# Two buffers for a turned tile, longer landing times in the plan, and a new order, in a kernel of four graph layers

## The chip, the cores and the metric

The kernel runs on one core of a Trainium2 chip. The metric is the device time of one execution in microseconds, the median of several runs. An execution that the hardware profiler recorded gives the profile; its own time is stated beside it.

## The reference

64 graphs of 256 nodes, each with 256 features in f32 and an integer adjacency matrix of 256 x 256. Four layers follow each other, and each ends in a residual sum and a layer norm. Cut to what is computed:

```python
# layer 0: attention with 8 heads over edges in either direction, then a feed-forward of width 1024
allowed = (adj > 0) | (adj.T > 0) | eye
q, k, v = split(x @ Wqkv.T + bqkv)
ctx = softmax(where(allowed, (q * scale) @ k.T, -inf)) @ v          # per head
x1 = layernorm(x + ctx @ Wo.T + bo)
y = layernorm(x1 + relu(x1 @ W1.T + b1) @ W2.T + b2)
x = layernorm(x + y)
# layers 1 and 2: graph attention, masked by adj (elu behind the second)
h = x @ W
e = leaky_relu(f[:, None] + g[None, :])                             # f = h @ a1, g = h @ a2
x = layernorm(x + softmax(where(adj > 0, e, -big)) @ h)
# layer 3: two graph convolutions over the edges of type 1, elu behind each
h = elu(x @ w_root + b + (adj == 1).T @ x / deg @ w_rel)            # twice
x = layernorm(x + h)
```

## The kernel before, in words

One graph is one unit of work: two tiles of 128 nodes. TensorE does the products, ScalarE exponentials and many evacuations of PSUM, VectorE masks, sums and statistics, POOL (GpSimd) a small root for each layer norm and DMAs that add, and SP (SyncE) issues the other DMAs.

**A plan sets the order of everything.** `main_path` doesn't issue instructions. It records operations in a `Plan`: setup as graph 0's first part, then `graph(g)` for each of the 64 graphs. Each operation has an engine, a cost in us, the tiles that it reads and writes and, on TensorE, a mode ("full", "row" for the 32-row score products, "col" for the values, "one" for gathering, "turn"). `Plan.schedule` then plays the operations through against these costs and puts them in order. An operation that moves data has a size and a `lag`, the time to landing. What is played decides only the order of issue; on the chip semaphores decide when things run.

**What the plan goes by.** Each kind of operation has a due time in `DUE`, and each graph a shift in `LATER`, about 41.12 us from one graph to the next; the sum is the operation's key. An engine takes, among its operations that are ready, the one with the smallest key. `WORTH` says how much the key is changed where a change of mode on TensorE would be saved or paid, `HOLD` how long TensorE may wait for a better operation, `WINDOW` how far ahead of its queue's head an operation may be taken. A pair of score groups is tied in `attention`: behind the first TensorE may be held for the second, for a time that `LOCK` sets. `RINGS` says how many buffers each kind of tile has; when all are in use the operation has to wait, in the plan and on the chip.

**How a tile is turned.** TensorE needs the features on the partitions. Except for the last five graphs, `bounced` does this without TensorE: VectorE transposes blocks of 32 x 32 into the tile `turned` (L839), SP sends that to DRAM (`rows`, L842, 256 KB, landing time `SENT` in the plan), and SP fetches it back in another order into a tile `T` (L847, landing time `BACK`). There are five such round trips in each graph: ahead of the feed-forward, of each attention layer and of each convolution. `turned` is free again once the send has landed. In the last five graphs `turned` is instead the scratch of a ScalarE copy (L828) ahead of a transpose on TensorE; in the first two graphs it serves the input. A column of the attention layers, f, is spread over all partitions in a like manner by `f_on_all`: `row<-cols` (L1102, `SENT_ROW`), then `pf<-row` (L1104, `BACK_ROW`), and VectorE uses it at L1134. `bits_bounced` turns the adjacency bits with the same two constants as `bounced`.

**Places that the steps touch.** The function `product`, at L888, issues all "full" products; the tile names tell them apart: `w,hid` is the second feed-forward product, `T,w` the first, `wo,ctxT` the output product, `gw,T` and `h,e` the attention layers, `cw,T` the convolutions. Scores are L1006, values L1041 and L1046, gathering L1208. PSUM has eight banks, a ring named `bank`: each product takes one, a score group takes four, and VectorE or ScalarE frees it by evacuating, for instance at L1067 behind the output product and the second feed-forward product.

Of the kernel before, what the change touches and what calls it, by code (L numbers as in the profile page):

```python
# [29 lines left out]
SENT, BACK = 2.5, 3.0  # L30
SENT_ROW, BACK_ROW = 2.7, 3.7
# [3 lines left out]
         "xr": 1, "hid": 1, "h": 3, "e": 3, "n": 1, "rel": 3, "hi": 2, "lo": 2, "o": 4, "blocks": 1, "turned": 1, "xT": 2, "cols": 2, "pf": 2, "turned_b": 1, "pt": 1}  # L35
# [4 lines left out]
WORTH, HOLD, WAIT, LOCK = 19.5, 0.38, 1000000.0, -0.5  # L40
WINDOW, FIRST, TAIL = 4.08, 6, 58
LANES = 8
DUE = [
    -3.32, 1.66, -76.45, -66.99, 176.19, 125.8, -337.49, 51.11, -306.84, 1289.72, 1238.75, 106.05, 1052.79, 157.6, 406.79, 32.53, 320.05, 308.78, 168.26, 372.3,
    359.81, 399.94, 414.94, 175.34, -771.48, 577.65, -163.58, 38.1, 102.4, 97.86, 212.59, 174.98, 232.55, 216.55, 274.84, 330.62, 335.24, 134.38, 316.14, 312.12,
    -714.12, 335.95, 93.11, 1673.19, 1202.97, 341.42, -15.89, 342.83, 413.55, 332.78, 471.02, 386.89, 1310.89, 1011.01, 864.41, 1559.09, 1349.75, 1637.58, 532.45, 391.77,
    408.67, 281.04, 416.08, 267.08, 455.95, 205, 355.16, 826.3, 430.38, 916.11, 855.23, 1541.74, 1480.45, 874.17, 97.88, -356.53, -611.17, -654.7, -556.93, 187.88,
    -58.31, -599.7, -1620.93, -1008.29, -941.93, 172.6, -1279.24, -1141.77, -510.52, -858.89, -979.24, -122.59, -551.6, -53.94, 320.94, 661.97, 122.99, 710.02, 442.1, 806.71,
    803.71, 196.79, 28.84, -268.67, 974.73, 412.51, 222.77, -44.51, 850.39, 787.86, 941.67, 355.66, -240.36, 390.1, 131.66, 324.9, -400.33, -177.96, -449.86, 87.86,
    479.23, 133.36, -458.92, 481.3, 336.71, 363.47, 57.85, -169.97, 1025.83, -703.56, 453.78, 429.72, -683.8, 94.09, -397.82, -779.14, -1443.53, -1281.14, -485.56, -330.59,  # L50
    -509.36, -1319.48, -919.17, -897.92, -285.58, -961.77, 42.95, 1101.45, 539.68, 510.97, -335.37, -103.6, -174.06, -1101.15, -1331.4, -1100.65, -427.55, -1096.38, -584.1, -528.48,
    302.19, -1032.08, -330.62, 813.25, 398.18, 877.77, 398.14, 1710.52, 243.46, -201.85, -604.71, 278.16, -763.26, -1414.9, -851.67, -2262.54, -1880.07, -2413.17, -1323.08, -993.79,
    -1535.67, -693.92, -857.19, -1680.81, -1238.83, -1544.75, -1551.8, -934.32, -665.58, 92.11, 250.88, 278.27, 1064.42, 556.25, 1200.96, 835.73, -229.1, 11.51, -1287.5, -719.39,
    491.11, -340.67, 297.98, 1036.71, 331.46, 935.5, 1276.44, 543.66, 635.98, -233.76, -236.54, -143.35, -85.56, 690.47, -1128.24, -188.51, 229.9, -337.83, -470.47, 303.07,
    294.95, -1177.63, -332.74, 497.93, 141.48, -1379, -1116.01, -852.76, -415.54, -805.34, -233.53, -85.67, -596.8, 398.69, 696.99, 36.47, 229.51, 513.36, 314.46, -844.71,
    -684.07, -952.69, -715.38, -939.59, -374.49, -1092.97, -2.92, -325.51, 48.64, 255.67, -499.52, -317.02, 498.86, 236.78, -987.53, -782.88, -696.09, -1493.47, 626.47, -425.51,
    328.26, 844.48, 40.56, -366.7, -664.35, -542.74, -715.91, -174.14, -819.33, -520.44, -852.66, 44.87, 87.36, -682.13, -510.83, 668.23, 127.3, -187.38, -1280.09, -1206.13,
    -1236.51, -626.27, -1017.5, -1329.36, -1426.82, -1567.82, -1426.23, -1356.52, -2016, -2549.52, -1764.4, -2044.6, -2365.67, -2132.03, -2998.04, -2021.84, -2693.01, -1477.56, -1450.67, -437.11,
    -1066.87, -1380.6, -1185.68, -1912.99, -1175.82, -162.05, -1388.62, -687.93, -841.24, -198.9, -255.02, 93.71, -418.45, -510.09, -139.81, 47.47, 135.24, 486.36, 940.09, 106.41,
    6.92, -142.92, -12.02, -979.84, -87.84, -965.42, -1781.15, -2113.16, -1887.77, -1185.84, -637.88, -1423.79, -566.06, -662.98, -128.84, -369.82, -195.94, -48.52, -1090.36, -444.68,  # L60
    -388.84, -151.83, 145.45, 234.1, 760.1, 257.54, -733.81, -429.47, 364.12, 792.5, -314.71, 646.77, -164.87, 701.44, 928.18, -19.63, 1261.73, 319.26, 612.03, 411.07,
    135.41, 335.64, -108.85, -486.71, -806.72, -566.65, -449.1, 43.21, -260.78, -477.86, -196.66, -58.56, 623.95, 663.12, -261.97, 184.16, -238.39, -199.48, 99.86, -71.13,
    -605.68, -363.77, -860.86, -278.1, 48.25, -322.31, -227.04, 52.9, -93.63, 752.97, -375.97, 104.87, 638.78, -464.01, 152.82, -357.39, -133.36, -172.46, -693.73, -319.61,
    -1412.19, -571.28, 21.04, -355.31, -767.51, -91.62, 338.07, -307.97, 256.87, 424.85, 725.57, -10.94, 461.61, -537.13, 230.24, 44.85, 169.31, -632.54, -605.49, 344.21,
    52.37, 61.16, -784.38, -840.31, -1510.97, -1387.71, -326.58, 0.5, -2.81, -445.54, -785.65, 159.28, -390.96, -339.72, -869.93, -460.79, -402.39, -246.94, -415.89, 172.83,
    17.22, 692.89, 140.89, 573.8, 162.6, 1080.8, 453.49, -61.94, 656.12, 203.45, 326.3, 632.37, 318.61, 358.35, 726.28, -221.2, 1220.66, 405.08, 364.19, -345.95,
    -118.89, -92.68, 12.95, -117.23, -118.43, 150.37, -31.48, 210.98, 66.46, 139.57, 130.65, 250.91, 77.66, 45.65, -90.38, 146.96, 120.09, 223.68, 302.85, 191.15,
    38.27, 121.41, 77.94, 257.82, 100.58, 94.11, 43.37, 414.45, 47.32, 244.3, 134.83, -56.21, 3.74, 101.61, 88.73, 107.62, 44.63, 75.98, 208.29, 120.2,
    76.84, 38.88, 124.51, -51.9, 57.61, -15.19, 219.49, 37.59, 238.22, 38.45, 165.9, 71.58, 103.5, 92.26, 36.02, 89.94, 114.24, 161.76, 136.12, 155.43,
    144.91, 136.25, 123.82, 173.19, 37.23, 54.94, 104, 351.37, 393.87, 420.97, 398.66, 329.73, 309.87, 376.83, 322.26, 357.45, 228.89, 342.28, 396.51, 264.8,  # L70
    409.7, 283.52, 331.27, 163.63, 197.2, 321.78, 181.03, 106.22, 172.35, 191.86, 363.79, 199.39, 154.03, 196.39, 365.08, 208.79, 166.91, 204.19, 148.9, 150.92,
    244.16, 201.73, 216.8, 205.05, 129.18, 306.33, 270.33, 298.69, 352.43, 242.1, 109.35, 149.21, -104.34, -63.72, 176.35, 97.62, 67.93, 247.43, 42.64, 224.12,
    197.04, 150.42, 99.42, 237.34, 203.98, 307.4, 319.2, 195.63, 311.24, 340.21, 420.84, 405.34, 295.63, 432.84, 393.88, 333.09, 378.89, 470.14, 353.74, 66.9,
    326.36, 491.34, 433.25, 443.86, 355.61, 304.99, 415.15, 458.93, 251.59, 519.13, 458.87, 384.71, 402.37, 377.98, 354.25, 449.89, 251.68, 289.09, 424.6, 414.09,
    405.23, 416.12, 379.79, 392.18, 370.61, 497.61, 394.33, 438.45, 405.63, 365.46, 396.94, 387.75, 400.37, 298.4, 408.37, 356.47, 404.89, 394.43, 352, 379.31,
    394.41, 251.56, 336.68, 302.2, 284.86, 400.44, 341.02, 509.96, 449, 481.19, 495.26, 517.82, 671.2, 389.86, 450.74, 491.74, 629.85, 444.94, 844.35, 203.63,
    11.32, 5.91, 0.56, 6.63, 27.83, 5.07, 14.09, 14.62, 28.08, 28.56, 51.27, 77.51, 59.49, 92.29, 98.75, 143.06, 30.76, 31.95, 39.6, 40.28,
    92.74, 93.6, 94.67, 95.03, 73.53, 76.62, 100.59, 105.53, 113.1, 113.3, 106.82, 109.59, 106.36, 108.11, 110.88, 116.61, 106.61, 107.98, 114.11, 109.72,
    111.49, 108.56, 113.73, 103.81, 119.66, 124.56, 124.37, 122.99, 122.52, 126.54, 125.24, 131.28, 134.46, 141.05, 142.97, 145.22, 145.49, 142.26, 209.5, 149.61,
    150.68, 151.53, 151.6, 152.66, 154.61, 171.25, 185, 155.74, 156.35, 160.25, 172.83, 187.04, 165.58, 166.44, 167.51, 166.87, 169.97, 172.59, 174.9, 174.38,  # L80
    173.45, 174.79, 175.86, 176.22, 167.3, 168.52, 174.02, 174.74, 177.85, 183.58, 187.56, 190.38, 196.2, 189.39, 200.1, 201.11, 203.16, 203.82, 201.61, 211.08,
    212.34, 221.15, 234.26, 238.23, 237.07, 238.97, 252.57, 296.8, 239.41, 241.4, 243.2, 250.85, 249.69, 251.34, 247.91, 253.96, 258.76, 258.67, 253.08, 254.17,
# [1444 lines left out]
```

## Time and profile before

| what | value |
|---|---|
| runs | 2748.38, 2755.47, 2757.27 us; median 2755.47 |
| profiled execution | 2746.21 us, span 2744.4 us |
| granted TensorE clock, mean | 0.995 |
| TensorE busy | 2695.8 us (98%), 15152 matmul records |
| VectorE busy | 2360.0 us (86%) |
| ScalarE busy | 1529.7 us (56%) |
| POOL busy | 1181.0 us (43%) |
| rows<-turned and T<-rows | 295 DMAs of 256 KB each |
| moved by DMA | 425.35 MB, 155 GB/s in the mean |

A stretch of the profile gives, for each engine, its busy time and in brackets its number of instructions. A group of waits gives the engine and line that waited, what ended the wait, the us in total, the times and the longest. The chain is the work that ended last, followed back from the end; in order of time each piece has its start, its length and what it was. A name such as `DMA pf<-row` in it is the time from a DMA's issue to its landing. "PEld" are TensorE's weight loads. A matmul of f32 leaves two records in the trace, so a score group of eight matmuls shows as x16.

### The profile page before, as it was taken

To read this page: it belongs to the slowest core of one execution; us is meant where nothing else is said; L and a number is where in the kernel's file an instruction comes from. 1 tells how busy PE (TensorE), PEld (TensorE's weight loads), DVE (VectorE), ACT (ScalarE), POOL (GpSimd) and SP (SyncE) were. 2 spreads that over 40 slices of the span, in tenths; PEclk is the share of its full clock that TensorE was granted. 3 is DMA by queue.
4 is the path that set the end of the run, shared out by engine and by line. 5 is a ranking of instruction groups with operands and counts; after the bars stand their busy time and mean duration, and the time that the engine had idled before them with its cause. 6 is when DMAs were issued, how large, how long until landed. Compare 5 with 4: busy or idle time off the path is not lost.

```text
span 2744.4 us, 48371 instructions
## 1 busy us (share of the span) xinstructions
PE 2695.8 (98%) x15152; PEld 2092.1 (76%) x15152; DVE 2360.0 (86%) x6585; ACT 1529.7 (56%) x3830; POOL 1181.0 (43%) x2051
## 2 busy tenths in 40 slices
PE   7999999999999999999999999999999999999997
PEld 5887777777777777777877777877777777777774
DVE  5688989889889898889898898898898898988767
ACT  4445555555555555555555555555555655556667
POOL 2443344344444444444444454444444444434222
PEclk9999999999999999999999999999999999999999
DMA  7786777577786786786776777777777877786221
GB/s 189 151 166 140 163 164 168 126 155 159 166 175 155 166 175 154 167 174 154 172 173 152 168 169 163 168 165 163 171 160 159 174 155 168 159 198 142 63 50 40
DMA packets 801742, 425.35 MB, mean 155 GB/s; under 512 B 552078, under 2 KB 777384, under 8 KB 801480
## 3 DMA queue, kind: packets, MB, share of 16 engines
q1 hardware_dynamic: 720504, 291.46, 41.1%
q0 software_dynamic: 80976, 130.72, 29.8%
q8 instruction: 124, 2.03, 0.3%
q14 instruction: 138, 1.13, 0.1%
HBM read 190.46 MB, written 102.09 MB: 107 GB/s over the span
## 4 chain that ended last, share of the span: by engine, by line
PE 65%; DVE 17%; DMA 9%; issue 3%; ACT 3%; POOL 2%; SPq 1%; DVEq 0%; ACTq 0%; POOLq 0%
PE bank L888 54%; DMA rows<-turned 4%; PE bank L1006 4%; DMA pf<-row 3%; PE bank L1208 3%; PE bank L1046 3%; DVE fold L1023 2%; DVE p L1014 2%; DVE turned L839 2%; PE bank L1041 1%; DVE e L1134 1%; DVE st L897 1%; ACT X L909 1%; DVE lo L1196 1%; DVE mv L899 1%
## 5 line engine op out<-in xcount | busy, mean ns | idle before, releaser
L902 POOL TENSOR_SCALAR rstd<-mv 128x2 f32<-128x2 f32 x384 | 135.9, 354 | 1041.2 <-DVE mv L899 918.0
L888 PE MATMUL bank<-T,w 128*128 128x256 f32 x2048 | 479.9, 380 | 1.1 <-DVE rdeg L1214 0.6
L888 PE MATMUL bank<-w,hid 128*128 128x256 f32 x2048 | 466.1, 382 | 1.8 <-ACT hid L1084 1.8
L888 PE MATMUL bank<-cw,T 128*128 128x512 f32 x1024 | 463.7, 593 | 2.6 <-DMA cw<-in_w_root_dram 1.1
L909 ACT ACTIVATE X<-X,rstd 128x256 f32<-128x256 f32 x640 | 350.1, 599 | 204.2 <-POOL rstd L905 196.0
L1012 ACT ACTIVATE p<-bank 128x512 f32<-128x512 f32 x512 | 300.4, 605 | 264.6 <-PE bank L1006 264.3
L888 PEld LDWEIGHTS bank<-w,hid 128*128 128x128 f32 x2048 | 396.3, 196 | 63.5 <-issue 21.5
L888 PEld LDWEIGHTS bank<-T,w 128*128 128x128 f32 x2048 | 382.5, 190 | 71.1 <-issue 21.8
L1014 DVE TENSOR_TENSOR p<-p,am 128x512 f32<-128x512 f32 x512 | 336.0, 679 | 8.8 <-ACT p L1012 8.0
L1084 ACT ACTIVATE hid<-bank,col_b 128x256 f32<-128x256 f32 x512 | 215.3, 472 | 225.7 <-PE bank L888 225.5
L888 PEld LDWEIGHTS bank<-cw,T 128*128 128x128 f32 x1024 | 198.3, 195 | 183.3 <-issue 164.6
L903 POOL TENSOR_TENSOR rstd<-rstd,neghalf 128x2 f32<-128x2 f32 x384 | 316.1, 823 | 32.3
L1029 POOL DMA_DIRECT2D fold<-p x240 | 204.9, 870 | 156.0 <-DMA fold<-p 65.8
L888 PE MATMUL bank<-xT,wqkv 128*128 128x256 f32 x1024 | 260.4, 383 | 1.2 <-DVE xT L880 0.8
L888 PE MATMUL bank<-h,e 128*128 128x259 f32 x1024 | 254.9, 382 | 2.6 <-ACT e L1139 0.9
L888 PE MATMUL bank<-gw,T 128*128 128x258 f32 x1024 | 254.1, 380 | 0.3 <-DMA T<-rows 0.3
L839 DVE STREAM_TRANSPOSE turned<-X 128x512 f32<-128x512 f32 x236 | 166.8, 707 | 101.8 <-DMA rows<-turned 86.9
L888 PEld LDWEIGHTS bank<-gw,T 128*128 128x128 f32 x1024 | 199.4, 195 | 49.3 <-issue 17.1
L897 DVE BATCH_NORM_STATS2 st<-X 128x6 f32<-128x256 f32 x640 | 234.5, 407 | 0.8
L888 PEld LDWEIGHTS bank<-h,e 128*128 128x128 f32 x1024 | 192.1, 190 | 38.1 <-issue 2.8
L888 PEld LDWEIGHTS bank<-xT,wqkv 128*128 128x128 f32 x1024 | 190.9, 191 | 32.8 <-issue 5.9
L1195 ACT CAST hi<-bank 128x256 fp32r<-128x256 f32 x256 | 93.1, 364 | 220.0 <-PE bank L888 219.2
(159 smaller groups left out, 4774.4 us busy)
## 6 DMA issues: line engine op xcount, KB each, us to landing
rows<-turned SPq DMA_DIRECT2D x295, 256.0 KB
T<-rows SPq DMA_DIRECT2D x295, 256.0 KB
fold<-p POOLq DMA_DIRECT2D x240, 256.0 KB, 5.0
adj<-in_adj_dram SPq DMA_DIRECT2D x128, 256.0 KB
x<-in_x_dram SPq DMA_DIRECT2D x64, 256.0 KB
xr<-in_x_dram SPq DMA_DIRECT2D x64, 256.0 KB
x<-row_bo POOLq DMA_DIRECT2D x64, 256.0 KB, 7.7
X<-row_b POOLq DMA_DIRECT2D x64, 256.0 KB, 6.5
```

The lines of the kernel that those rows point to most:

```text
L839: dve(0.63, lambda: nc.vector.transpose(turned().rearrange("p k (b n i) -> p (k b) i n", b=4, i=NB), xt().rearrange("p i (j c) -> p j i c" ...
L888: nc.tensor.matmul(dst, lhsT=lhs(c), rhs=rhs(c), start=(c == 0), stop=(c == n - 1))
L897: nc.vector.bn_stats(stat()[:, i, :], y()[:, i, :])
L902: nc.gpsimd.tensor_scalar(rstd()[:, 0, :], mv()[:, :, 1], 1.0, EPS, op0=ALU.mult, op1=ALU.add)
L903: nc.gpsimd.tensor_tensor(rstd()[:, 0, :], rstd()[:, 0, :], neghalf[:, 0:NB], op=ALU.pow)
L909: nc.scalar.activation(y()[:, i, :], y()[:, i, :], AF.Identity, bias=rstd()[:, 1, i : i + 1], scale=rstd()[:, 0, i : i + 1])
L1006: nc.tensor.matmul(s[r]()[:, hg, :], lhsT=qk()[f, KB + hg, kt * P : (kt + 1) * P], rhs=qk()[f, hg, :], start=True, stop=True)
L1012: act(0.58, lambda pr=pr, k=k, sr=s[r]: nc.scalar.activation(pr(), sr(), AF.Exp, accum_out=seen_sum[:, k : k + 1]), [s[r]], [(p[kt], r)])
L1014: dve(0.60, lambda pr=pr, kt=kt: nc.vector.tensor_tensor(pr(), pr(), am()[:, kt, None, :].to_broadcast([P, KB, N]), op=ALU.mult), [(p[kt], ...
L1029: op("POOL", 1.3, lambda kt=kt, hg=hg, into=into, out_of=out_of: nc.gpsimd.dma_start(fold()[into], p[kt]()[out_of, hg], accum_op=ALU.add), ...
L1084: act(0.36, lambda f=f, k=k, ph=ph: nc.scalar.activation(hid()[:, f + k, :], ph()[:, k, :], AF.Relu, bias=b1[:, f + k : f + k + 1]), [ph, ...
L1195: act(0.27, lambda i=i, po=po: nc.scalar.copy(hi()[:, i, 0:D], po()[:, D:]), [po], [(hi, i)])
```

## The change

The ring of `turned` gets two buffers in place of one. The landing times that the plan uses grow: `SENT` from 2.5 to 3.5 us, `BACK` from 3.0 to 4.0, `SENT_ROW` from 2.7 to 3.0, `BACK_ROW` from 3.7 to 5.0. `WORTH`, `HOLD` and `WINDOW` get other values, and all of `DUE` (one number for each kind of operation) and `LATER` (one for each graph) are replaced. No function changes. The core of the diff:

```diff
-SENT, BACK = 2.5, 3.0
-SENT_ROW, BACK_ROW = 2.7, 3.7
+SENT, BACK = 3.5, 4.0
+SENT_ROW, BACK_ROW = 3.0, 5.0
...
-         "xr": 1, "hid": 1, "h": 3, "e": 3, "n": 1, "rel": 3, "hi": 2, "lo": 2, "o": 4, "blocks": 1, "turned": 1, "xT": 2, "cols": 2, "pf": 2, "turned_b": 1, "pt": 1}
+         "xr": 1, "hid": 1, "h": 3, "e": 3, "n": 1, "rel": 3, "hi": 2, "lo": 2, "o": 4, "blocks": 1, "turned": 2, "xT": 2, "cols": 2, "pf": 2, "turned_b": 1, "pt": 1}
...
-WORTH, HOLD, WAIT, LOCK = 19.5, 0.38, 1000000.0, -0.5
-WINDOW, FIRST, TAIL = 4.08, 6, 58
+WORTH, HOLD, WAIT, LOCK = 18.26, 0.66, 1000000.0, -0.5
+WINDOW, FIRST, TAIL = 3.87, 6, 58
...
 DUE = [
-    -3.32, 1.66, -76.45, -66.99, 176.19, 125.8, -337.49, 51.11, -306.84, 1289.72, 1238.75, 106.05, 1052.79, 157.6, 406.79, 32.53, 320.05, 308.78, 168.26, 372.3,
+    -5.24, 61.16, -55.48, -121.71, 131.27, 116.42, -360.14, -13.03, -412.23, 1303.25, 1202.5, 122.94, 1220.77, 264.52, 518.37, 26.62, 302.48, 323.95, 108.43, 382.73,
...
 LATER = [
-    -295.85, -398.08, 82.34, 186.95, 93, 148.02, 240.73, 287.76, 328.96, 370.08, 411.2, 452.32, 493.44, 534.56, 575.68, 616.8, 657.92, 699.04, 740.16, 781.28,
+    -295.77, -316.139, 89.742, 180.353, 93.824, 148.535, 242.616, 290.067, 328.968, 370.089, 411.21, 452.331, 493.452, 534.573, 575.694, 616.815, 657.936, 699.057, 740.178, 781.299,
...
```

## The prediction

> **What bounds the kernel now.** I read the page first, then the windows of the stages, then the chain that ended last in order of time, then the waits of TensorE and of VectorE, and last the timeline of TensorE at the places that these name.
>
> The page:
>
> ```profile
> PE 2695.8 (98%) x15152; PEld 2092.1 (76%) x15152; DVE 2360.0 (86%) x6585; ACT 1529.7 (56%) x3830; POOL 1181.0 (43%) x2051
> ```
>
> TensorE is busy for all but 48.6 us of the span. "Busy" takes in matmuls that were issued and stand in the pipe, so this alone doesn't say that nothing is lost. The stages (columns PE, PEld, DVE, ACT, POOL, then clock, DMA share, GB/s):
>
> ```profile
> 34.10:529.00 494.90, 487.47 (x2868) 384.58 (x2868) 406.91 (x1095) 262.64 (x668) 205.23 (x357) 0.99 0.76 158
> 529.00:2104.70 1575.70, 1571.93 (x8818) 1227.10 (x8817) 1407.38 (x3904) 867.63 (x2233) 724.76 (x1210) 1.00 0.75 165
> 2104.70:2594.70 490.00, 482.40 (x2727) 369.49 (x2726) 423.08 (x1179) 287.17 (x706) 203.60 (x367) 1.00 0.71 153
> 2594.70:2744.40 149.70, 133.70 (x653) 96.03 (x652) 110.58 (x366) 102.31 (x197) 41.11 (x102) 0.97 0.20 45
> ```
>
> In the steady stretch (529 to 2104.7) TensorE idles 3.8 us, VectorE is busy for 89%, and nothing else is near. The idle time lies in the filling (7.4 us after the first 34), the emptying (7.6) and the last 150 us (16.0). The chain in order of time shows what the steady stretch still loses; the 20.94 us piece is the same eighty matmuls in every graph, so its starts are the clock of a period:
>
> ```profile
> 1118.12 20.94 PE bank L888 x80
> ...
> 1159.25 20.94 PE bank L888 x80
> ...
> 1224.69 6.01 DMA pf<-row
> 1236.05 3.99 DMA rows<-turned
> 1242.53 20.93 PE bank L888 x80
> ...
> 1283.65 20.94 PE bank L888 x80
> ```
>
> The undisturbed period is 41.12 us (1283.65 less 1242.53). From 1159.25 to 1242.53 two periods took 83.28, so 1.04 more, and there the chain leaves TensorE: a row of f that came back late (pf), then a turned tile whose buffer was still being sent, then VectorE. Over the whole stretch the same piece starts at 619.65 and, 36 periods later, at 2114.39: 41.52 a period. So 0.40 us a period, 14.4 us in 36, is lost to waits. Where they end (waits of the weight loads, 540 to 2200):
>
> ```profile
> PEld bank L1006 <- DVE X L1067: 8.9, 12, 1.4
> ```
>
> and VectorE's own waits in the steady stretch (us in total, times, longest):
>
> ```profile
> DVE turned L839 <- DMA rows<-turned: 65.6, 40, 3.2
> DVE e L1134 <- DMA pf<-row: 39.3, 34, 3.5
> DVE o L1224 <- ACT e L1223: 28.3, 37, 0.9
> ```
>
> The score matmuls (L1006) wait for a bank that VectorE has yet to empty at L1067. VectorE is late because it stood 65.6 us for its one `turned` buffer and 39.3 us for pf. The timeline shows the place: the pair of score groups with such a wait, a group alone twice, and a pair without a wait:
>
> ```profile
> 782.33 1.57 PE L1006 MATMUL bank<-qk 32*128 32x256 f32 x22
> 784.54 1.12 PE L1006 MATMUL bank<-qk 32*128 32x256 f32 x10 [0.64 <-DVE X L1067]
> 785.60 1.99 PE L888 MATMUL bank<-wo,ctxT 128*128 128x256 f32 x8
> ...
> 2192.61 1.15 PE L1006 MATMUL bank<-qk 32*128 32x256 f32 x16
> 2193.68 3.73 PE L888 MATMUL bank<-w,hid 128*128 128x256 f32 x16
> 2197.34 1.15 PE L1006 MATMUL bank<-qk 32*128 32x256 f32 x16
> 2198.42 1.78 PE L888 MATMUL bank<-wo,ctxT 128*128 128x256 f32 x7
> ...
> 2553.64 2.01 PE L1006 MATMUL bank<-qk 32*128 32x256 f32 x32
> 2555.59 0.70 PE L888 MATMUL bank<-wo,ctxT 128*128 128x256 f32 x2
> ```
>
> From start to the next group's start: 3.27 us with the wait, 1.95 for a pair without one, 1.07 and 1.08 for single groups.
>
> **The change part by part.** No instruction is added or taken away; the built program of after has the same matmuls, VectorE operations and DMAs, in another order.
>
> *The order on TensorE.* Before repeats one order of a period 38 times: values (L1041, L1046), half of the second feed-forward product, both score groups, the output product. After repeats another one 41 times: values, one score group, half of that product, the other score group, the output product. This is the pattern that before shows once, at 2192.61. A split pair costs 1.07 + 1.08 - 1.95 = 0.20 to 0.21 us. The score matmuls stand in 83 runs in before and in 125 in after, 42 more: 42 x 0.21 = +8.8 us, all on the path, since TensorE is it. The runs of the other kinds stay (64 of values, 171 against 175 of gathering, 28 against 27 of transposes).
>
> A rule speaks here too. The Trainium skill, "TensorEngine Tiling (Array Packing)", section Key Properties, says that changing the tiling mode drains TensorE; "TensorE: Matmul & The Clock Gate", section "Step-by-step: what each phase is for", puts a drain at about 128 cycles, which at its 2.4 GHz is an estimate of 0.05 us. After has one change of mode more in a period, so 42 x 0.05 = 2.2 us by the pages against 8.8 by the trace. I take the trace.
>
> *What the split does to the wait.* In before the bank of the second half of the feed-forward product goes to the second score group, with one score group between (1.08 us), and emptying it takes 0.68 us of VectorE (51.71 us for 76 at L1067) plus the hand-over. Some tenths are left, and any lateness of VectorE shows. In after that bank goes to a matmul with 4.6 us of TensorE work between. Counting the same way for every bank in after's period, the shortest distance behind a VectorE eviction is 3.5 us, and the shortest at all 1.7 us, behind two ScalarE copies of hid (2 x 0.47 us); before had 2.2 us there and no wait. So the 14.4 us should go but for a small rest, which I set at 0.05 us a period: -12.4.
>
> *The second `turned` buffer.* In before only 1.8 us of VectorE work lies between two turns at the tightest place of a period, while a send takes 4 us (3.99 above), so VectorE must stand. In after, with two buffers, the turn that could meet a send in flight comes 5.65 us of VectorE work later or more. The 65.6 us go from VectorE. The skill's page "Trainium Kernel Development and Optimization", section Best Practices, says to double-buffer so that DMA and compute overlap; read as a gain in time that would be 65.6 us. The trace disagrees: TensorE doesn't wait for VectorE but for the 0.40 us a period already counted, so on top of it the buffer is worth nothing. If that cover goes, and VectorE is the later one, up to 65.6/38 = 1.7 us a period is what it protects.
>
> *Longer landing times.* They only move orders. The send of a turned tile was planned at 0.5 + 0.9 + 2.5 = 3.9 us, as measured; after plans 4.9, which is spare. pf was planned at 0.5 + 0.45 + 3.7 = 4.65 and took 6.0 here; after plans 5.95. Yet VectorE's order leaves about 8.8 to 10 us of its own work between the column and its use, as before (9.3 to 10.1), so I expect most of the 39.3 us of pf waits to stay, covered by the larger distances on TensorE. The distances on the transposes' round trips: 17.3 us of TensorE work (15.6 before, without a wait) ahead of the feed-forward, 21.1 (28.7 before) ahead of the second attention layer, 25.3 (22.5) ahead of the second convolution. The shortened one is closest to new trouble: its chain is 0.5 evicting, 1.2 statistics, 1.8 POOL, 1.2 scaling, 0.7 turning, 4.0 sending, about 3.5 back, 12.9 us in sum, which leaves 8 us for queueing.
>
> *SP, POOL, ScalarE.* The same DMAs in another order on two queues. SP waits 325.9 us for rows<-turned in before, ahead of everything behind it; a send that may go out before the former one is fetched back can only loosen that. POOL's adding DMAs and ScalarE (43% and 56% busy) I cost at nothing, covered by the distances above; a late fold would stop the values, which have 33 us in both orders.
>
> *Filling and emptying.* Both are searched anew and I can't read their waits from before. Bounds: all 7.4 us of the filling gained, or as much lost; likewise 7.6 and 16.0 at the end. Distances behind the round trips are a little longer in after's filling, so I take -3.5 there; at the end there are as many tight places in one as in the other (output products 2.7 and 4.4 us behind their values, against 3.6 and 3.7), so 0.
>
> Sum on the profiled execution: 8.8 - 12.4 - 3.5 = -7.1, so 2746.2 to 2739.1 us. The three runs shown are 2748.4, 2755.5 and 2757.3: the profiled one is 9.3 below their median. If those 9 us are waits of this kind, after's distances save some; I take 3 of them. So -10 on the median: 2745.
>
> **The rivals.**
>
> *The pair is split and the wait stays* (slower). VectorE remains late because pf still stops it, and the wait moves to another bank. Then +8.8 stands alone: 2764. It decides at 0.21 us of wait a period (below it the order gains) and reaches 0.3% at the full 0.40. For it: 39.3 us of pf waits and 28.3 us for ScalarE stay. Against it: bank distances of 3.5 us and more. If the shortened round trip (21.1 us) also failed by 0.5 us a period, 20 us more.
>
> *A wash.* The split eats what the wait gave, filling and emptying are as before: 2755.5 + 8.8 - 12.4 = 2752. For it: all terms are measured on before except the filling.
>
> *More than counted.* The ordinary runs lose more than the profiled one in the same waits and the ends improve by half of their idle time: -20, 2735. For it: the 9 us between them.
>
> *The change doesn't do what it says*, because TensorE was the bound throughout: that is the wash, since the buffer relieves VectorE alone.
>
> **How the numbers follow.** What can be told from no change is about 0.3%, 8.3 us: under 2747.2 is faster, over 2763.7 slower. My forecast 0.38, the wash 0.26, more than counted 0.13, the wait that stays with what may come on top 0.23. Nearly all of the forecast case lies below 2747.2 or close to it (0.33 below, 0.05 above), so faster is 0.46, same 0.05 + 0.22 + 0.02 = 0.29 (the wash but for 0.04 that ends slower, and 0.02 of the staying wait), slower 0.25. The range takes in all but the ends: 2731 to 2767. The likeliest case alone is 2738 to 2750.
>
> **What would show it.** In the chain of after, the undisturbed period should be about 41.33 us instead of 41.12, and the mean within 0.1 of it (41.52 before); single score groups at 1.08. "DVE turned <- DMA rows<-turned" should all but vanish, "DVE e <- DMA pf<-row" stay at 25 us or more, and "L1006 <- DVE X L1067" be gone from TensorE's waits. A mean period above 41.5, or a new line in TensorE's waits in the steady stretch (T<-rows ahead of gw, hid ahead of a gathering), would make it wrong; so would a filling or an emptying whose idle time moves by more than 8 us.

## The result, and the profile after

The changed kernel takes 2733.52 us (median of 4 runs, 2730.40 to 2736.22). The kernel before, run beside it on the same chip, takes 2753.18 us (4 runs, 2748.38 to 2757.27). The ratio is 0.9929, with a 95% interval of 0.9908 to 0.9950: faster by 19.7 us. The profiled executions took 2730.4 and 2746.2 us, spans 2728.6 and 2744.4, at the same mean granted clock of 0.995; they differ by 15.8 us.

The page, busy time of each engine:

```profile
PE 2697.2 (99%) x15152; PEld 2081.2 (76%) x15152; DVE 2343.2 (86%) x6585; ACT 1561.6 (57%) x3830; POOL 1139.6 (42%) x2051
```

The same instructions, and TensorE's idle time is down from 48.6 to 31.4 us. The windows of the stages (PE, PEld, DVE, ACT, POOL, then clock, DMA share, GB/s):

```profile
34.10:529.00 494.90, 489.59 (x2892) 386.71 (x2884) 408.63 (x1098) 263.25 (x673) 201.08 (x357) 0.99 0.78 161
529.00:2104.70 1575.70, 1575.66 (x8817) 1216.36 (x8817) 1396.08 (x3909) 901.12 (x2238) 688.29 (x1208) 1.00 0.78 165
2104.70:2594.70 490.00, 489.76 (x2796) 377.61 (x2796) 427.45 (x1206) 294.77 (x716) 203.01 (x376) 1.00 0.71 150
2594.70:2728.60 133.90, 119.12 (x520) 83.87 (x519) 98.20 (x325) 91.65 (x176) 38.70 (x93) 0.96 0.19 44
```

In the steady stretch and in the emptying TensorE now idles 0.04 and 0.24 us, where it was 3.8 and 7.6. That looks like a gain in the steady stretch. It isn't one, and only the chain of waits in order of time shows it. The piece of one hundred matmul records of L888, which runs from the output product to the first gathering, marks the period here:

```profile
1146.25 1.08 PE bank L1006 x16
1147.33 3.66 PE bank L888 x16
1150.99 1.07 PE bank L1006 x16
1152.06 25.39 PE bank L888 x100
...
1193.52 25.39 PE bank L888 x100
...
1234.97 25.39 PE bank L888 x100
```

A period is 41.46 us nearly every time, with no DMA and no VectorE in the chain. Before it was 41.12 where nothing disturbed it, and 41.47 in the mean once the disturbances are counted. So the waits in the chain are gone, and the undisturbed period has grown by as much. VectorE's largest wait in the steady stretch (what waited, what ended it: us in total, times, longest):

```profile
DVE X L1067 <- PE bank L888: 89.0, 75, 1.3
```

VectorE has turned from the late one into the early one: it now waits at L1067 for TensorE's product (89.0 us; 7.4 before), and waits neither for the sending of `turned` (65.6 before) nor for `pf` (39.3 before). What the weight loads of the score groups wait for in the same stretch:

```profile
PEld bank L1006 <- DVE e L1134: 14.0, 34, 0.4
```

The score groups no longer wait for the bank of L1067. What is left is 0.4 us at a time of a weight load, which overlaps running matmuls. The list for "PE" itself is empty in this stretch.

To see where the time came from, I cut every trace at the same piece of work instead of at the same microsecond: the start of the values (L1041) of the 1st, 14th, 52nd and 64th graph. The times of the pieces in us, with the runs of the experiments below; "period" is the constant period in the steady stretch, or the mean one:

| kernel | to the 1st | filling, 1st to 14th | steady, 14th to 52nd | emptying, 52nd to 64th | rest | period |
|---|---|---|---|---|---|---|
| before | 34.1 | 494.9 | 1575.7 | 490.0 | 149.7 | 41.12 undisturbed, 41.47 mean |
| after | 31.9 | 490.0 | 1575.8 | 478.0 | 152.9 | 41.46 |
| e1: after's order, one buffer | 32.5 | 508.8 | 1592.4 | 487.0 | 153.2 | 41.46 undisturbed, 41.9 mean |
| e2: before's order, two buffers | 33.9 | 491.3 | 1562.9 | 485.4 | 149.8 | 41.12 |
| e3: before's dates, two buffers, planned anew | 35.0 | 507.7 | 1588.5 | 499.9 | 159.5 | 41.53 to 41.55 |
| e4: after's dates, old landing times | 32.5 | 559.6 | 1577.5 | 525.6 | 137.0 | 41.46 |
| e7: as e2, own buffer for one turn only | 35.3 | 495.8 | 1563.0 | 486.0 | 149.8 | 41.12 |
| e8: as e2, but not for that turn | 34.0 | 491.4 | 1578.4 | 486.4 | 149.8 | 41.12 to 42.98 |
| e9: as e2, split pair | 36.3 | 494.9 | 1571.6 | 481.9 | 149.7 | 41.33 |
| e10: before, split pair, one buffer | 35.6 | 496.7 | 1572.3 | 489.9 | 149.9 | 41.33 |
| e11: as e3, longer landing times | 35.6 | 528.5 | 1634.7 | 514.6 | 162.0 | 42.90 |

From before to after the pieces change by -2.2, -4.9, +0.1, -12.0 and +3.2 us, in sum -15.8. The steady stretch, nearly three fifths of the time, gave nothing. The -12.0 us of the emptying are the one large gain.

### The profile page after: what moved, and what is told of

It reads as the page before. It is cut to its first block, busy times and chain, and to the rows that moved or that the text cites. A ratio compares the mean times of both kernels' runs of the same rounds, so it can differ in the third digit from the quotient of the medians.

```text
span 2728.6 us, 48260 instructions
## 1 busy us (share of the span) xinstructions
PE 2697.2 (99%) x15152; PEld 2081.2 (76%) x15152; DVE 2343.2 (86%) x6585; ACT 1561.6 (57%) x3830; POOL 1139.6 (42%) x2051
## 4 chain that ended last, share of the span: by engine, by line
PE 93%; DVE 3%; DMA 2%; ACT 1%; issue 1%; SPq 0%; POOL 0%; POOLq 0%; DVEq 0%; ACTq 0%
PE bank L888 78%; PE bank L1006 5%; PE bank L1208 4%; PE bank L1046 4%; PE bank L1041 1%; DMA pf<-row 1%; DMA wqkv<-in_WqkvT_dram 1%; DMA T<-rows 0%; DVE p L1014 0%; PE bank L817 0%; SPq L877 0%; DMA fold<-p 0%; DVE st L897 0%; PE bank L763 0%; DVE fold L1023 0%
## 5 line engine op out<-in xcount | busy, mean ns | idle before, releaser
L902 POOL TENSOR_SCALAR rstd<-mv 128x2 f32<-128x2 f32 x384 | 117.6, 306 | 984.2 <-DVE mv L899 838.9
L888 PE MATMUL bank<-cw,T 128*128 128x512 f32 x1024 | 470.4, 593 | 1.0 <-ACT hid L1084 0.9
L888 PE MATMUL bank<-T,w 128*128 128x256 f32 x2048 | 468.4, 381 | 1.3 <-DVE ctxT L1056 0.6
L888 PE MATMUL bank<-w,hid 128*128 128x256 f32 x2048 | 466.1, 382 | 0.0
L888 PEld LDWEIGHTS bank<-w,hid 128*128 128x128 f32 x2048 | 392.8, 196 | 56.9 <-issue 17.2
L888 PEld LDWEIGHTS bank<-T,w 128*128 128x128 f32 x2048 | 385.9, 191 | 57.0 <-issue 3.4
L1014 DVE TENSOR_TENSOR p<-p,am 128x512 f32<-128x512 f32 x512 | 333.4, 675 | 14.3 <-ACT p L1012 13.4
L888 PEld LDWEIGHTS bank<-cw,T 128*128 128x128 f32 x1024 | 198.2, 195 | 163.6 <-issue 150.6
L903 POOL TENSOR_TENSOR rstd<-rstd,neghalf 128x2 f32<-128x2 f32 x384 | 285.3, 743 | 32.3
L888 PE MATMUL bank<-gw,T 128*128 128x258 f32 x1024 | 262.7, 381 | 1.4 <-issue 1.1
L888 PE MATMUL bank<-h,e 128*128 128x259 f32 x1024 | 257.7, 384 | 0.2 <-ACT e L1139 0.2
L1084 ACT ACTIVATE hid<-bank,col_b 128x256 f32<-128x256 f32 x512 | 209.1, 468 | 78.8 <-PE bank L888 77.0
L888 PE MATMUL bank<-xT,wqkv 128*128 128x256 f32 x1024 | 245.6, 382 | 0.9 <-ACT xT L867 0.7
L888 PEld LDWEIGHTS bank<-gw,T 128*128 128x128 f32 x1024 | 199.5, 196 | 48.9 <-issue 26.9
L888 PEld LDWEIGHTS bank<-xT,wqkv 128*128 128x128 f32 x1024 | 193.1, 190 | 34.1 <-issue 5.6
L888 PEld LDWEIGHTS bank<-h,e 128*128 128x128 f32 x1024 | 187.2, 189 | 39.5 <-issue 14.8
```

What stands on the lines that cost most here:

```text
L888: nc.tensor.matmul(dst, lhsT=lhs(c), rhs=rhs(c), start=(c == 0), stop=(c == n - 1))
L902: nc.gpsimd.tensor_scalar(rstd()[:, 0, :], mv()[:, :, 1], 1.0, EPS, op0=ALU.mult, op1=ALU.add)
L903: nc.gpsimd.tensor_tensor(rstd()[:, 0, :], rstd()[:, 0, :], neghalf[:, 0:NB], op=ALU.pow)
L1014: dve(0.60, lambda pr=pr, kt=kt: nc.vector.tensor_tensor(pr(), pr(), am()[:, kt, None, :].to_broadcast([P, KB, N]), op=ALU.mult), [(p[kt], ...
L1084: act(0.36, lambda f=f, k=k, ph=ph: nc.scalar.activation(hid()[:, f + k, :], ph()[:, k, :], AF.Relu, bias=b1[:, f + k : f + k + 1]), [ph, ...
```

## The experiments

The change has three parts: a buffer, a plan's constants, an order. The experiments ran in three groups, each on one chip: e1 to e4, e5 to e8, e9 to e11. My theory while reading the result: the second buffer alone takes the wait away, and the new order gives the gain of the steady stretch back. The rival is the prediction's: the new order's longer distances between a bank's eviction and its next use take the wait away, and the buffer adds nothing to that.

**e1: the order of after with one buffer.** Up to the 52nd graph all turned tiles use one buffer; a send goes out just before the next turn into the same buffer (that part of the edit is left out here).

```diff
-            self.at = self.plan.rings[self.ring][1](self.shape, self.dtype, self.slot)
+            self.at = self.plan.rings[self.ring][1](self.shape, self.dtype, 0 if self.only else self.slot)
...
-                x = NB * 32
+                x, turned.only = NB * 32, g < 52
```

> After's order, but the five turned tiles of graphs below 52 all use one buffer; where a turn stood ahead of the send of the tile before it, that send is issued just ahead of the turn. TensorE's order stays after's. Theory A (the order carries the gain, the second buffer only keeps VectorE free, and TensorE has distances of 3.5 us and more to it): VectorE's waits for rows<-turned come back and are larger than the 65.6 us of before, since one turn now follows another after 0.9 us of VectorE work, some 100 us in the steady stretch; TensorE's period stays within 0.15 us of after's 41.46, and the time is +2 to +8 us on after. Rival B (the second buffer carries the gain): VectorE's 35 us of work and 3 us of waits a period leave no slack, the wait reaches TensorE in most periods, +0.4 us a period or more, and the time is back at before's or above it (+16 us and more).

Measured: 2776.26 us, ratio 1.009 (1.0062 to 1.0117), 39 to 43 us above after. VectorE's waits in the steady stretch:

```profile
DVE turned L839 <- DMA rows<-turned: 79.0, 32, 4.2
...
DVE turned L839 <- ACT p L1012: 26.1, 7, 5.0
```

and TensorE's:

```profile
PE bank L888 <- DVE ctxT L1056: 14.6, 14, 1.9
```

After's order lets two turns follow each other with only 0.9 and 4.1 us of VectorE work between, against sends of about 4 us. It cannot do without the second buffer: the steady stretch loses 16.6 us, and the filling 18.8. Without the buffer VectorE's lateness does reach TensorE, at the output product behind `ctxT`, in spite of the longer bank distances.

**e2 and e6: the order of before with two buffers.** The plan still counts on one buffer, so that every instruction stays where it was; on the chip consecutive turned tiles alternate between two.

```diff
-        def ring(name, bufs):
-            plan.ring(name, bufs, lambda shape, dtype, i: pools["work"].tile(shape, dtype, tag=f"{name}{i}", name=name))
+        def ring(name, bufs, turns=iter(range(10**6))):
+            plan.ring(name, bufs, lambda shape, dtype, i: pools["work"].tile(shape, dtype, tag=f"{name}{next(turns) % 2 if name == 'turned' else i}", name=name))
```

> Before's order and plan unchanged on every engine; the turned tiles alternate between two buffers. Theory A: VectorE's 65.6 us of waits for rows<-turned go, so the score pair is delayed less often; but pf is still late (39 us of waits), so of the 0.40 us a period half stays: mean period 41.3, time -5 to -8 us on before, with filling and emptying as in before. Rival B (the second buffer carries the gain): mean period 41.15, time as after's or below it, -14 to -20 us. Rival C (pf alone delays VectorE where it matters): period stays at 41.45 to 41.52, within 2 us of before.

> Before's order, turned tiles alternating between two buffers, a second time, beside after. Theory F: 22 to 28 us below before and 5 to 10 us below after. Rival G: no difference from after.

Measured: 2726.11 us (ratio 0.991, 0.9885 to 0.9935) and, taken again, 2724.89 us (0.9899, 0.9878 to 0.9920). This is the best kernel of the study: e6 is 12.0 us below the changed kernel on the same chip (e5), e2 7.4 us below its first runs. It is more than either expectation had allowed. The chain in order of time:

```profile
1107.03 1.94 PE bank L1006 x32
1108.97 20.94 PE bank L888 x80
...
1150.07 20.93 PE bank L888 x80
```

A pair of score groups without a wait, and 41.10 us from one to the next. VectorE's waits in the window of the steady stretch:

```profile
DVE X L1067 <- PE bank L888: 59.6, 37, 2.3
DVE e L1134 <- DMA pf<-row: 40.1, 32, 3.6
```

The wait for `pf` is as large as before (39.3), and so is the one for ScalarE (29.2 against 28.3), and both cost nothing once the wait for `turned` is gone. Whether `pf` on time would have done as well alone was not tried: in the chain of before a late row and a late turn stand together ahead of a late L1067. The 1.08 us between the bank's eviction and its use, which the prediction held to be the trouble, are enough when VectorE is on time.

**e7 and e8: which of the five turns.** In before's order the turn ahead of the first convolution (`layer == 0` below) follows the turn ahead of the second convolution, of an earlier graph, after 1.8 us of VectorE work. In e7 only the turn ahead of the first convolution has a buffer of its own; in e8 all turns alternate but that one, which stays in the buffer of the turn before it. The edit of e7:

```diff
-            self.at = self.plan.rings[self.ring][1](self.shape, self.dtype, self.slot)
+            self.at = self.plan.rings[self.ring][1](self.shape, self.dtype, 1 if self.other else self.slot)
...
-                hT, hT_at = rearranged(h)
+                which[0] = layer == 0; hT, hT_at = rearranged(h); which[0] = False
```

> Before's order; of the five turns of a graph only that ahead of the first convolution, which follows the turn before it after 1.8 us of VectorE work, has a buffer of its own; the other four share one. Theory F with its mechanism (a send takes 4 us, so the wait arises where the turns stand less than that apart, at this one place): VectorE's waits for rows<-turned fall from 65.6 us in the steady stretch to under 10, the period is 41.12 to 41.2, the time within 4 us of two alternating buffers. Rival H (the lateness is spread over the turns, those at 4.3 and 4.7 us too): half of the gain at most.

> Before's order; the turned tiles alternate between two buffers, but the turn ahead of the first convolution must take the buffer of the turn just before it. Theory F with its mechanism: VectorE's waits stay at 60 us or more, the period at 41.4 to 41.55, the time within 5 us of before. Rival H: half of the gain or more.

Measured: e7 2730.14 us (0.9918, 0.9896 to 0.9940), e8 2746.74 us (0.9986, 0.9970 to 1.0002: no change that can be told from none). VectorE's largest wait in e8:

```profile
DVE turned L839 <- DMA rows<-turned: 63.9, 38, 3.1
```

and TensorE's, which e7 no longer has:

```profile
PE bank L1006 <- DVE X L1067: 4.8, 9, 1.2
```

One buffer for one turn carries the whole gain of the steady stretch (1563.0 us against 1562.9), and two buffers for the four other turns carry none of it (1578.4 against 1575.7). The wait is one place in each graph, not five. On the whole e7 is 5.2 us above e6, where 4 had been allowed; its profile is longer in the filling and the emptying, not in the steady stretch.

**e9 and e10: the split pair by itself.** One due time of before is set 4 us earlier. With it the plan puts the first score group ahead of half of the second feed-forward product and leaves the rest of the period on TensorE as it was, in 32 graphs in a row. VectorE's order moves with it, which matters below. e9 has two alternating buffers as e2 has, e10 the one buffer of before.

```diff
-    92.74, 93.6, 94.67, 95.03, 73.53, 76.62, 100.59, 105.53, 113.1,
+    92.74, 93.6, 94.67, 95.03, 73.53, 76.62, 100.59, 101.53, 113.1,
...
```

> The order of before with two alternating turned buffers, and one due time 4 us earlier, so that in 32 graphs in a row the first score group runs ahead of the half feed-forward product, the second behind it, and nothing else on TensorE is moved there. The prediction's first term (a split pair costs 1.07 + 1.08 - 1.95 = 0.21 us): a constant period of 41.12 + 0.21 = 41.33 us in these graphs, so 0.13 us of the 0.34 by which the changed kernel's period of 41.46 exceeds 41.12 belong to something else in its order. Rival one, the split is the whole 0.34: 41.46. Rival two, the split costs nothing where VectorE is on time: 41.12. On the time: 32 x 0.21 = 7 us above 2725 with the first, but the order at the end changes too, so the period decides.

> The same order with the one turned buffer of before. The prediction's second step (the longer distance between a bank's eviction and its next use removes the wait, the buffer adds nothing): VectorE still stands about 60 us for its turned buffer, no wait for L1067's eviction remains on TensorE, and the mean period in the 32 graphs is 41.33 to 41.38 us. The theory that only the second buffer removes the wait: the lateness passes to another place, and the mean period is 41.33 + 0.40 = 41.7 us.

Measured: e9 2735.52 us (0.9925, 0.9903 to 0.9947), e10 2744.16 us (0.9963, 0.9949 to 0.9977). The chain of e10, two starts of the same piece:

```profile
1113.33 1.07 PE bank L1006 x16
1114.40 3.66 PE bank L888 x16
1118.06 1.08 PE bank L1006 x16
1119.14 20.94 PE bank L888 x80
...
1160.47 20.94 PE bank L888 x80
```

and of e9:

```profile
1117.99 20.94 PE bank L888 x80
...
1159.33 20.94 PE bank L888 x80
```

Both have 41.33 to 41.34 us in nearly all periods (e10 has one of 41.44 and one of 42.03). So the split costs 0.21 us, whether or not VectorE is on time, and it takes the wait from TensorE even with one buffer. Among VectorE's waits of e10 between 560 and 1850 us:

```profile
DVE turned L839 <- DMA rows<-turned: 18.1, 24, 2.2
```

VectorE still stands for `turned`, but in the same window before had 57.2 us of it, 32 times, and I had expected about 60 us here. It shrinks because VectorE's order has changed too: a mask product (L1014) now stands between the two turns, and VectorE spends a part of the time there, waiting for ScalarE.

```profile
DVE p L1014 <- ACT p L1012: 19.1, 24, 1.1
```

Besides, the half product that L1067 evicts now ends one score group later (1.08 us), so VectorE is there first more often. In the same window of e10, and then of before:

```profile
DVE X L1067 <- PE bank L888: 28.2, 28, 1.6
...
DVE X L1067 <- PE bank L888: 4.5, 10, 1.5
```

So e10 changes three things at once: TensorE's distances, the end of that product, and VectorE's order. They can be told apart only where VectorE is late. Record by record, in 33 periods from the 14th graph on, L1067 of the second half product started more than 0.1 us later than the product allowed in 17 periods of before and in 4 of e10. In before 16 of the 17 periods grew by just that lateness, less 0.05 to 0.08 us: that is all the slack the old order has there. In e10 the lateness was 0.22, 0.23, 0.52 and 1.13 us, no score group waited, and the periods grew by 0.01, 0.01, 0.11 and 0.70, further on in the period. So the prediction's distance does take the wait off the score pair, but it is seen at work in four periods; in the others VectorE was on time.

The steady stretch of e10 is 1572.3 us, 3.4 below before. My theory was too narrow: there are two cures for the same wait. The buffer takes it away at 41.12 us a period, the split with what it moves on VectorE at 41.33. After has both and needs to pay for one.

The remaining 0.13 us (41.46 less 41.33) belongs to something else in after's order. Record by record, one place differs. Behind the products of `T,w` the first record of `h,e` starts 0.27 us after the one before it, and the next 0.29 after that, where the records around them are 0.22 apart: 0.12 in sum. The weight loads of after there, by group and then in order of time, and VectorE beside them:

```profile
L888 PEld LDWEIGHTS bank<-h,e x4: 186/190/192, 1176.3 to 1176.8; 128*128 128x128 f32 x4
...
L888 PEldq EVENT_SEMAPHORE  x1: 51/51/51, 1176.2 to 1176.2; - x1
...
1176.31 0.74 PEld L888 LDWEIGHTS bank<-h,e 128*128 128x128 f32 x4 [0.26 <-issue]
...
1175.80 0.39 DVE L1198 TENSOR_TENSOR o<-bank,row_cb 128x256 f32<-128x256 f32 x1
```

An instruction of 51 ns that does nothing but wait stands between. It is not a cost in itself: between two products before has 315 of them in 36 graphs, and behind 307 the products follow at their usual distance. Here it marks a wait for VectorE. L1198, which empties a convolution's bank, ends 0.04 us before it starts, in each of 36 graphs of after and likewise in e1, e4 and e5, and by the trace's semaphores L1198 is what ended it. So after's order has a bank wait of its own. The lists of waits put it down to "issue", and TensorE counts as busy through it. No run has moved L1198.

**e3, e4 and e11: landing times and due times.** e3 is before with two buffers in the plan too, e11 adds the longer landing times, both with before's due times. e4 is after with the old landing times.

```diff
e3, e11:
-... "turned": 1, ...
+... "turned": 2, ...
e11:
-SENT, BACK = 2.5, 3.0
-SENT_ROW, BACK_ROW = 2.7, 3.7
+SENT, BACK = 3.5, 4.0
+SENT_ROW, BACK_ROW = 3.0, 5.0
e4 (from after):
-SENT, BACK = 3.5, 4.0
-SENT_ROW, BACK_ROW = 3.0, 5.0
+SENT, BACK = 2.5, 3.0
+SENT_ROW, BACK_ROW = 2.7, 3.7
```

> Before with the ring of turned at two, planned anew with before's due times and landing times: the score pair stays together, one place of the period changes. Theory A: as the run with before's order and two buffers, within 4 us. Rival D (due times that were searched for one buffer are spoilt by any replanning, above all at both ends, since the order repeats 31 times instead of 38): 5 to 15 us above before.

> After with before's four landing times, planned anew with after's due times: the pattern of the period is after's but for one place, and it repeats 36 times instead of 41. Theory A (the search, not the landing times as such, gives the order; the times only decide how far a send is believed): within 4 us of after. Rival E (the longer landing times protect TensorE from late transfers): TensorE waits for T<-rows or VectorE for pf again in the steady stretch, 0.2 us a period or more, +8 us and more on after.

> Before with two turned buffers in the plan and the longer landing times of the changed kernel, planned with before's due times. Without the longer landing times the same gave 2788.7 us, stages of 507.7, 1588.5 and 499.9 us. If longer landing times are a gain in themselves, this comes out clearly lower, below 2770 us. If due times and landing times only fit each other as they were searched, it stays at or above 2788 us, with the loss at filling and emptying and a steady period of 41.5 us or more.

Measured: e3 2788.72 us (1.0135, 1.0111 to 1.0159), e4 2832.77 us (1.0285, 1.0257 to 1.0313), e11 2872.12 us (1.042, 1.0396 to 1.0443). All are slower than before: each plays due times against constants that they were not searched with. e3 is 38 us above before, where 15 had been the most expected; e4 is 96 to 99 above after, and not by waits in the steady stretch, where they had been expected. In e4 the steady period stays at 41.46 us, and the filling loses 69.6 us against after. TensorE's waits there, from 34 to 600 us:

```profile
PE bank L888 <- DMA T<-rows: 37.2, 11, 10.1
```

A plan that takes a transfer for shorter than it is calls products that are not there yet. In e11 VectorE's wait for `pf` falls to 7.3 us (10 times), which is what a longer landing time is for, but the period grows to 42.90, because new waits come up on TensorE itself, this one the longest:

```profile
PE bank L1208 <- DVE lo L1196: 28.7, 31, 1.5
```

So longer landing times are no gain in themselves, nor is a second buffer in the plan; in after they go with due times searched for them. Which of the two made after's filling and emptying better can't be read from these runs.

**e5: after once more,** on the chip of e6, e7 and e8.

> The kernel after, on the same chip as the three runs below. Theory F, formed on the first four runs (the second buffer carries the whole gain, and after's order gives a part of it back in every period: 41.46 us against 41.12): 18 to 22 us below before and 5 to 10 us above the run with before's order and two buffers. Rival G (after's order is worth as much at both ends as it loses in the period): within 3 us of it.

Measured: 2736.87 us (0.9938, 0.9917 to 0.9959): 14.8 us below before and 12.0 above e6, where 18 to 22 and 5 to 10 had been expected. Stages 33.5, 495.1, 1575.9, 477.5 and 153.2 us. The steady stretch and the emptying repeat to within 0.5 us; the filling differs by 5.1 between the two profiled executions of after, as much as its supposed gain. e2 and e6 are within 3.1 us of each other in each stage.

## Why the prediction was right, and where it was not

The forecast was 2745 us, 10 below the median of before; measured are 19.7 below the median of the runs beside it, and 14.8 when taken again (e5). Direction and range hold, but in part by luck. The sum had -3.6 us from the split and the wait together, and the steady stretch gave +0.1. It had nothing from the end, and the emptying gave -12.0. Both measured medians lie under the likeliest case (2738 to 2750). The rival "more than counted" (2735) was nearest in the number and named the ends, though not the cost in the steady stretch.

*The split pair, +8.8 us.* Right, and it is the one term that was tested alone: e9 has 41.33 against 41.12, the 0.21 that single groups of 1.08 and a pair of 1.95 gave. Costing it by the row of the trace (0.21) rather than by the drain that the Trainium skill gives in "TensorE: Matmul & The Clock Gate", section "Step-by-step: what each phase is for" (an estimate of 0.05), was the better choice: e9's 0.21 is four times that estimate.

*The wait in the score pair, -12.4 us, by the order's distances.* The size is right (13 us: the whole 0.34 to 0.40 a period went). The mechanism is there (e10's four late periods), but e10 reached 41.33, the period predicted for after, mostly with VectorE on time. The slack of the old order is 0.05 to 0.08 us, where the prediction had some tenths. Distance isn't the only cure, and in after the buffer had already removed the cause.

*The second buffer, "worth nothing on top".* This is the step that failed. The prediction saw both effects, priced the order first and the buffer second, and never asked what the buffer would do in the old order. The runs give that: 1575.7 to 1562.9 us in the steady stretch, and 24 to 27 us on the whole (e2, e6, each against the median of before beside it). The order, taken second, costs: e2 to after is -2.0, -1.3, +12.9, -7.4 and +3.1 us over the five pieces, +5.4 in sum with rounding, and the 12.9 are 38 periods times 0.34. Side by side on one chip, e6 to e5 is -0.1, +3.4, +11.9, -4.8 and +3.3, +13.7 in sum. It was right that the buffer protects something: e1 loses 39 to 43 us, under the bound of 65.6. It was right too that 65.6 us of VectorE's waiting are not a gain of 65.6 us; what TensorE felt of them was a fifth (12.8).

*What the prediction did not have: 0.13 us a period.* Every cost but the split was set at nothing for the new order on TensorE, since no bank was nearer than 3.5 us behind VectorE's eviction. That count is of TensorE's work and leaves out when VectorE comes to the eviction: L1198 ends just as TensorE needs its bank. So the predicted period of 41.33 came out as 41.46, 5 us over the steady stretch, and the mean wasn't within 0.1 us of it. A mean above 41.5, which would have made the forecast wrong, was missed by 0.04 us.

*`pf`, "stay at 25 us or more".* Wrong in after: the wait is gone. It mattered to nothing, for e2 runs at 41.12 us with 40.1 us of it. The first rival (the wait passes to another bank, 2764 us) rested on these waits and falls with that; a wait for another bank did come, L1198's, but at 0.13 us a period, under the 0.21 at which that rival would have turned the gain.

*Filling -3.5, emptying 0.* Start and filling gave 7.1 us in the first profile of after and 0.4 in the second (e5). The emptying gave 12.0, and the last piece took 3.2 back. TensorE's waits from 2080 to 2600 us in before:

```profile
PE bank L1006 <- DVE X L1067: 2.8, 3, 1.5
PE bank L888 <- DVE ctxT L1056: 2.2, 2, 1.3
PE bank L888 <- DMA T<-rows: 1.0, 2, 0.8
```

and all that is left of them in after:

```profile
PE bank L888 <- DMA T<-rows: 0.2, 1, 0.2
```

The idle 7.4 us were the bound that I had written down and then set to nothing, on a count of tight places. Of the 12.0 us, 4.6 come with the buffer alone in e2 and 7.6 in e6, and the rest, about 4 to 7, with the new plan. This is where after is better than e2, and the only place that could be worth taking over; which of its waits the new plan removes by what was not tried.

*The 3 us for ordinary runs* came out at 3.9: the medians differ by 19.7 us and the profiled executions by 15.8.

## What to carry to other kernels

Before an order is searched anew for a new resource, give the old order the resource without telling the planner, one place at a time. Here a second buffer at one of five turns was the gain of the steady stretch, and the search on top of it gave that stretch's gain back. Follow a wait to the engine that sets the time: of 65.6, 39.3 and 28.3 us of waiting on VectorE, taking away the first was enough, the other two then cost nothing, and none of the totals said so. And read the undisturbed period beside the idle time: after's TensorE idles 0.04 us in 1576 and still is no faster there.

## What the runs showed of the hardware that was not expected

Splitting a row of sixteen score matmuls (32 rows, 256 columns, f32) into two rows of eight costs 0.21 us, with the operands there in time (e9, every one of 32 periods within 0.07 us). A wait for a bank can also stay below what the lists of waits show: behind L1198, which ended 0.04 us before, two records in a row came about 0.05 and 0.08 us late in every graph of after, 0.13 us in the median. TensorE counts as busy all that time.
